# A delta-rule layer with attention and a routed feed-forward: expert gates sent along with the scattered rows, gathers that add, row counts by matmul, softmax sums in PSUM, and a new table of leads

## The chip, the cores and the metric

One core of one Trainium2 chip. The time is device microseconds of one execution of the whole kernel, a median over several runs; one further execution is profiled.

## The reference, cut to what matters

Input x has 4 sequences of 1024 tokens of 128 channels. All arithmetic is float32.

```python
# first half: gated delta rule, 16 heads of 8 channels
q, k, v = silu(depthwise_conv4(silu(x @ W.T)))     # q and k are l2-normalised
a, b = sigmoid(x @ Wa.T), sigmoid(x @ Wb.T)
for t in tokens:                                    # a scan over 1024 steps
    S = a*S - a*b*outer(S @ k, k) + b*outer(v, k)
    o[t] = q @ S
x = layernorm(x + o @ Wo.T)
# second half, on the result
ctx = softmax over the 4 sequences, per token and head   # attention length 4
x   = layernorm(src + ctx @ out_w.T)
probs = softmax(x @ gate_w.T)                       # 8 experts
topv, topi = top_k(probs, 2); topv /= topv.sum()
y = sum over the two chosen e of topv[e] * (relu(x @ w1[e].T + b1[e]) @ w2[e].T + b2[e])
x = layernorm(x + y); x = layernorm(src + x)
```

(Biases are left out; `src` is the result of the first half. The last line stands for the layer norm of the expert part and the residual around the second half.) An expert has 128 inputs, 512 hidden units and 128 outputs.

## The kernel before, in words

The 1024 tokens are cut into 8 chunks of 128 tokens; a chunk holds the same 128 tokens of all four sequences, so most tiles are 128 partitions by 4 x 128 numbers. Each chunk passes through the stages `project` (q, k, v and the gates), `prepare` (convolution, norms, and the triangular solve inside blocks of 8 tokens), `recur` (16 serial steps, one per block), `output`, `attend` (up to the softmax, lines 1325 to 1354), `attended` (the rest of the attention, routing, and the shared part of the result), and `experts`. `experts` runs over the groups (0, 1), (2, 3), (4, 5), (6), (7) of chunks.

One step of `recur` is four VectorE instructions (L1095, L1101, L1110, L1116), with one ScalarE activation (L1107) that the third of them waits for; step n+1 begins with the result of step n, in PSUM.

`attended` makes for each chunk a mask of the two chosen experts per token, the gates `g2`, and `rank`: with one matmul against a triangular matrix the number of earlier tokens of the same sequence that chose each expert (L1455), and with one against ones the number in the whole chunk (L1456), both for each of the four sequences. It also writes `base`, the part of the result that needs no expert, to DRAM (`base_kept`).

`experts` works out for every token and choice a row in a DRAM table `sorted` that has each expert's tokens together, rounded up to tiles of 128 rows: it adds the totals of the sequences (L1500, L1505), derives the first row of each expert, and walks over the sequences, adding `first` to the ranks (L1543) and the sequence's total to `first` (L1545). Eight indirect DMAs per chunk (L1555, on GpSimd's queue) scatter the rows of `x2`, the normalised tokens, into `sorted`. Then it goes over the tiles, four at a time: load four tiles (L1566), transpose them (L1571), apply the layer norm's gain (L1573, `xlT`), and for each tile load the weights of its expert, 514 KB (L1586, three buffers), four matmuls into PSUM `ph` (L1596), four activations into `h` (L1605), four matmuls into PSUM `pm` (L1609). After four tiles one ScalarE copy takes `pm` to `yl` (L1617), which is stored in the DRAM table `ys` (L1618). `ph` and `pm` have one bank each. At the end, per chunk, `acc` is loaded from `base_kept` (L1623), eight indirect DMAs gather rows of `ys` into a buffer `yg` (L1627), and after each one VectorE does acc = yg * gate + acc (L1633). Two layer norms (lines 1244 to 1252), a gain (L1644) and a residual (L1647) follow, and the store of the output.

The order in which each engine gets its instructions is not that of the program. The kernel is built twice: the first time a planner (`plan`, `forward`) gives every instruction a cost and a rank, runs a list schedule over the five queues, and keeps the order; the second time this order is imposed. The rank is the length of the longest chain behind an instruction, plus a number from the table `LEAD`, one for every 60 instructions of a stage. The delay from the end of an instruction to one on another engine is taken from the table `HOP`. Where the planner sees a hole on TensorE, it puts in matmuls whose result is not used (L612), to keep its clock up. DMAs other than the indirect ones are issued by SyncE (SP), in its planned order.

Of the kernel before, what the change touches and what calls it, by code (L numbers as in the profile page):

```python
# [51 lines left out]
T = 128  # L52
# [9 lines left out]
E, F = 8, 512  # L62
# [3 lines left out]
NT = 2 * B * T * GROUP // P + E - 1  # L66
STEPS = B * T * GROUP // P
Q = 4
# [16 lines left out]
class Slots:  # L85
# [32 lines left out]
PE_, DVE_, ACT_, POOL_, SP_ = range(5)  # L118


HOP = (
    (0.0, 0.054, 0.053, 0.054, 0.05, 0.044),
    (0.038, 0.0, 0.033, 0.034, 0.04, 0.03),
    (0.037, 0.035, 0.0, 0.04, 0.04, 0.05),
    (0.09, 0.08, 0.063, 0.0, 0.06, 0.07),
    (0.031, 0.028, 0.026, 0.027, 0.0, 0.017),
)

OVERLAP = (0.0, 0.083, 0.11, 0.043, 0.0)

# [1 line left out]

PIECE = 60
LEAD = (
    (-596, -698,),
    (-695,),
    (1215, 1142,),
    (-239,),
    (-326,),
    (42, 327,),  # L140
    (-717, -154,),
    (-605, -1049,),
    (-810,),
    (-141, -914,),
    (-468,),
    (847, 645,),
    (142, 371,),
    (832, -867,),
    (-1488,),
    (-525, 14,),  # L150
    (21,),
    (154, 573,),
    (-536, 239,),
    (150, -335,),
    (-139, 302, 1084, 833, 618, 867, 306, -62, 535,),
    (-103,),
    (-319, 358,),
    (21,),
    (822, 1113,),
    (325, 133,),  # L160
    (-330, -211,),
    (-341,),
    (-499, -431,),
    (-273,),
    (809, 430,),
    (21, 79,),
    (510, -110,),
    (-99, 422, 15, 260, -43, 347, -211, 876, 125,),
    (-488,),
    (97, -532,),  # L170
    (-438,),
    (334, 1061,),
    (82, -55,),
    (-748, -468,),
    (-347,),
    (-566, -206,),
    (-890,),
    (673, 244,),
    (-525, -84,),
    (-74, -848,),  # L180
    (330, -102, -426, -699, -279, -40, -524, 453, 218,),
    (-566,),
    (129, -1199,),
    (-377, -137,),
    (-533, 514,),
    (378, 91, 339, 237, 165, 545,),
    (172,),
    (-80, 3,),
    (-409, -393, 106, 565, -698, 771,),
)  # L190
WINDOW, DOWN, UP = 3.413, 0.39, 0.77
FILL, FILL_MIN, FILLER = 0.7, 0.5, 0.225
TABLES = {"Silu": 1, "Sigmoid": 2, "Exp": 3}


# [221 lines left out]
def forward(units, rank):  # L417


    q = Queue(units, [u.preds for u in units], rank)  # L420
# [4 lines left out]
    for _ in units:  # L425
# [62 lines left out]
        for s in u.succs:  # L488
            v = units[s]
            if v.engine != e or transfer:  # L490
                q.release(s, end + HOP[v.engine][5 if transfer else e])
            else:
                q.release(s, end if k in v.waits and e != PE_ else begin)
    return begin_, end_, order, holes


# [98 lines left out]
def delta_moe_kernel(  # L595
# [176 lines left out]

    sorted_rows = []
    for n in range(2):
        t = nc.dram_tensor(f"sorted{n}", (NT * P, C), F32).ap()

        sorted_rows.append((t, dram_disjoint_views(t, GROUP * 2 * B)))

    def clear_sorted():
        zero = tile2k("zero", "yl", 2).rearrange("p s c -> p (s c)")  # L780
        nc.vector.memset(zero, 0.0)
        for t, _ in sorted_rows:
            for i in range(0, NT, 4):
                m = min(4, NT - i)
                nc.sync.dma_start(
                    t[i * P : (i + m) * P].rearrange("(i p) c -> p i c", p=P),
                    zero[:, 0 : m * C].rearrange("p (i c) -> p i c", c=C),
                )


# [485 lines left out]
    def attend(c):  # L1276
# [46 lines left out]
        for s in range(B):  # L1323
# [7 lines left out]
                MUL,  # L1331
            )
            prods.append(prod)
        ps = psum.tile([P, B, T // 2], F32, tag="pc", name=f"ps_sc{c}", bufs=1)
        for s in range(B):
            for f in range(2):
                nc.tensor.matmul(  # L1337
# [10 lines left out]
            sc, ps, mx[:, None, :].to_broadcast([P, B, T // 2]), SUB  # L1348
        )
        nc.scalar.activation(sc, sc, AF.Exp, scale=float(DH) ** -0.5)  # L1350
        den = small([P, T // 2], f"den{c}")
        nc.vector.tensor_reduce(den, sc.rearrange("p s t -> p t s"), AX.X, ADD)
        nc.vector.reciprocal(den, den)
        nc.vector.tensor_tensor(
# [4 lines left out]
    def attended(c):  # L1359
# [35 lines left out]
        x2 = tile2k(f"x2_{c}", "x2", 3)  # L1395
# [85 lines left out]
        routed[c] = (x1_kept, base_kept, x2, best, g2, rank)  # L1481

    def pick(best, out, t, name):
        chosen = small([P, 2, B, E], name)
# [5 lines left out]
    def experts(group):  # L1490
# [3 lines left out]
        nt = 2 * B * T * len(group) // P + E - 1  # L1494


        n_e = small([P, E], f"ne{g0}")
        for i, (_, _, _, _, _, rank) in enumerate(members):
            if i == 0:
                nc.vector.tensor_reduce(  # L1500
                    n_e, rank[:, 1].rearrange("p s e -> p e s"), AX.X, ADD
                )
            else:
                more = small([P, E], f"more{g0}")
                nc.vector.tensor_reduce(  # L1505
                    more, rank[:, 1].rearrange("p s e -> p e s"), AX.X, ADD
                )
                nc.vector.tensor_tensor(n_e, n_e, more, ADD)
# [28 lines left out]

        xs, views = sorted_rows[groups.index(group) % 2]
        rows_of_ = []
        for i, (_, _, x2, best, _, rank) in enumerate(members):  # L1540
            where = rank[:, 0]
            for s in range(B):
                nc.vector.tensor_tensor(where[:, s], where[:, s], first, ADD)  # L1543
# [17 lines left out]
        ys = dram.tile([NT * P, C], F32, tag="ys", name=f"ys{g0}")  # L1561
        for i0 in range(0, nt, Q):
            m = min(Q, nt - i0)
            part = slice(i0 * P, (i0 + m) * P)
            xl = tile2k(f"xl{g0}_{i0}", "xl", 2)
            nc.sync.dma_start(  # L1566
                xl[:, 0:m], xs[part].rearrange("(i p) c -> p i c", p=P)
            )
            ps = psum.tile([P, Q, P], F32, tag="ph", name=f"ps_xl{g0}_{i0}", bufs=1)
            for i in range(m):  # L1570
                nc.tensor.transpose(ps[:, i, :], xl[:, i, :], ident)  # L1571
# [45 lines left out]
            nc.scalar.copy(yl[:, 0:m], ps_y[:, 0:m])  # L1617
            nc.sync.dma_start(  # L1618
                ys[part].rearrange("(i p) c -> p i c", p=P), yl[:, 0:m]
            )  # L1620
        for c, (x1_kept, base_kept, _, _, g2, _), rows_at in zip(group, members, rows_of_):
            acc = tile2k(f"acc{c}", "acc", 2)
            nc.sync.dma_start(acc, base_kept)  # L1623
            for g in range(2):
                yg = tile2k(f"yg{c}_{g}", "yg", 1)
                for s in range(B):
                    gp.indirect_dma_start(  # L1627
                        yg[:, s, :],
                        None,
                        ys[0 : nt * P, :],  # L1630
                        bass.IndirectOffsetOnAxis(ap=rows_at[:, g, s : s + 1], axis=0),
                    )
                    nc.vector.scalar_tensor_tensor(  # L1633
                        acc[:, s, :],
                        yg[:, s, :],
                        g2[:, g, s : s + 1],
                        acc[:, s, :],
                        MUL,
                        ADD,
                    )  # L1640
# [198 lines left out]
```

## Time and profile before

| | |
|---|---|
| median of 3 runs | 833.56 us (831.26 to 834.96) |
| the profiled execution | 832.78 us |
| its span, first to last instruction | 831.1 us |
| busy: TensorE (PE) | 699.4 us, 84% of the span |
| busy: VectorE (DVE) | 564.6 us, 68% |
| busy: ScalarE (ACT) | 412.8 us, 50% |
| busy: GpSimd (POOL) | 475.4 us, 57% |
| granted TensorE clock, mean | 0.953 |
| moved | 139.67 MB, mean 168 GB/s |
| last step of the last `recur` | ends at 566 us |
| last matmul of the last expert tile | ends at 802.5 us |

Busy time is that in which an engine has at least one instruction under way; matmuls that only keep the clock up count. PEld is TensorE's loading of weights, which overlaps its matmuls. A float32 matmul leaves two records.

### The profile page before, as it was taken

The numbers are of one execution on the slowest core, as the hardware profiler recorded it, in microseconds if no ns is written. First come the engines' busy times: TensorE is split into PE (matmuls) and PEld (weight loads), VectorE is DVE, ScalarE is ACT, GpSimd is POOL, SyncE is SP. The second block draws the span as 40 slices with busy tenths as digits, with TensorE's granted clock in tenths as the row PEclk, the third lists the DMA queues.
The fourth block names the chain that finished last, engine by engine and source line by source line (L and its number), as shares of the span: only waits on it lengthen the run. The fifth ranks groups of instructions, "written<-read, shape, count | busy, mean of one in ns | idle before, by whom it ended". The sixth has DMA issues, their size and how long they took to land. (4 is left out here: it accounts for less than half of the span.)

```text
span 831.1 us, 15634 instructions
## 1 busy us (share of the span) xinstructions
PE 699.4 (84%) x5000; PEld 516.5 (62%) x5000; DVE 564.6 (68%) x1742; ACT 412.8 (50%) x1163; POOL 475.4 (57%) x656
## 2 busy tenths in 40 slices
PE   8989797889985988999889888799898999977750
PEld 5555545456553673667677577577477878777640
DVE  2167897898977998989899888987426351531303
ACT  5246362555653435486456435455325565465531
POOL 3534339849646748846746987653778621662213
PEclk9999999999997999999989999999899999999995
DMA  7642244252425245378458648568268688788741
GB/s 204 172 136 85 90 128 130 79 178 79 127 89 156 75 148 171 104 218 264 147 175 279 192 124 249 151 193 264 87 203 231 215 231 256 229 243 258 210 124 29
DMA packets 120070, 139.67 MB, mean 168 GB/s; under 512 B 9517, under 2 KB 90933, under 8 KB 119989
## 3 DMA queue, kind: packets, MB, share of 16 engines
q1 hardware_dynamic: 115893, 130.29, 52.0%
q0 software_dynamic: 4096, 8.40, 3.6%
q8 instruction: 39, 0.64, 0.3%
q14 instruction: 42, 0.34, 0.1%
HBM read 99.53 MB, written 39.12 MB: 167 GB/s over the span
## 5 line engine op out<-in xcount | busy, mean ns | idle before, releaser
L1605 ACT ACTIVATE h<-ps_ph,w_e 128x128 f32<-128x128 f32 x396 | 115.0, 368 | 91.2 <-PE ps_ph L1596 46.8
L1609 PE MATMUL ps_pm<-w_e,h 128*128 128x128 f32 x792 | 134.8, 296 | 19.9 <-ACT h L1605 18.6
L1609 PEld LDWEIGHTS ps_pm<-w_e,h 128*128 128x128 f32 x792 | 110.7, 193 | 39.8 <-ACT h L1605 34.9
L1596 PE MATMUL ps_ph<-xlT,w_e 128*128 128x128 f32 x792 | 116.8, 287 | 8.2 <-ACT xlT L1573 4.4
L1596 PEld LDWEIGHTS ps_ph<-xlT,w_e 128*128 128x128 f32 x792 | 101.1, 196 | 21.2 <-ACT xlT L1573 9.3
L897 PE MATMUL ps_pa<-z,diag 128*128 128x512 f32 x192 | 94.3, 620 | 7.8 <-ACT conv L906 3.0
L1627 POOL DMA_INDIRECT yg<-dr_ys,rows_at x64 | 62.2, 972 | 56.1 <-DMA dr_ys<-yl 26.9
L1555 POOL DMA_INDIRECT sorted<-x,rows_at x64 | 63.3, 989 | 49.9 <-DVE rows_at L1551 20.1
L1107 ACT ACTIVATE p<-ps_su,g_block 128x32 f32<-128x32 f32 x127 | 40.3, 317 | 98.4 <-DVE ps_su L1101 95.9
L1201 POOL TENSOR_TENSOR out_work<-sc__0_704,qg_r 128x512 f32<-128x512 f32 x64 | 73.4, 1165 | 14.3 <-PE ps_po L1205 5.7
L1633 DVE SCALAR_TENSOR_TENSOR acc<-yg,g2x,acc 128x128 f32<-128x128 f32 x64 | 24.0, 379 | 72.1 <-DMA yg<-dr_ys,rows_at 71.9
L1110 DVE TENSOR_TENSOR p<-ps_su,kd_r 128x256 f32<-128x256 f32 x127 | 53.1, 418 | 19.2 <-ACT p L1107 18.8
L897 PEld LDWEIGHTS ps_pa<-z,diag 128*128 128x128 f32 x192 | 33.9, 194 | 43.7 <-issue 30.3
L1101 DVE TENSOR_REDUCE ps_su<-z 128x32 f32<-128x288 f32 x128 | 58.1, 454 | 1.9
L1095 DVE TENSOR_TENSOR z<-ps_su,wt 128x256 f32<-128x256 f32 x128 | 53.4, 417 | 8.5 <-ACT su_out L1133 3.9
L1116 DVE TENSOR_REDUCE ps_su<-p 128x32 f32<-128x288 f32 x127 | 57.5, 453 | 1.6
L1173 POOL TENSOR_TENSOR out_work<-uc,q_r 128x192 f32<-128x192 f32 (+3 forms) x64 | 51.0, 827 | 12.3 <-DMA uc<-dr_su_back 11.8
L1219 POOL TENSOR_TENSOR out_work<-k_r,qu 128x128 f32<-128x128 f32 (+6 forms) x64 | 50.7, 818 | 7.8 <-DVE o L1227 5.3
L1086 ACT COPY z<-x 128x32 f32<-128x32 f32 x128 | 30.7, 245 | 38.7 <-DVE ps_su L1101 38.3
L940 POOL TENSOR_TENSOR work<-conv 128x320 f32<-128x320 f32 (+6 forms) x56 | 36.0, 666 | 22.4 <-DVE x L1035 19.5
L1035 DVE TENSOR_REDUCE x<-work 128x128 f32<-128x256 f32 (+6 forms) x56 | 45.5, 812 | 1.2 <-ACT work L1026 0.3
L1252 ACT ACTIVATE acc<-acc,le_nm,le_rs 128x128 f32<-128x128 f32 x64 | 28.1, 496 | 34.0 <-DVE le_nm L1250 34.0
(209 smaller groups left out, 1481.6 us busy)
## 6 DMA issues: line engine op xcount, KB each, us to landing
w_e<-in_wp SPq DMA_DIRECT2D x99, 514.0 KB, 4.7
dr_bounce<-conv SPq DMA_DIRECT2D x24, 256.0 KB, 2.4
xl<-sorted SPq DMA_DIRECT2D x21, 256.0 KB, 3.2
dr_ys<-yl SPq DMA_DIRECT2D x21, 256.0 KB, 5.0
kd_r<-dr_bounce SPq DMA_DIRECT2D x16, 256.0 KB, 3.1
work<-dr_bounce SPq DMA_DIRECT2D x16, 256.0 KB, 4.5
dr_su_back<-su_out SPq DMA_DIRECT2D x8, 512.0 KB
sorted<-yl SPq DMA_DIRECT2D x10, 256.0 KB, 4.3
```

The source lines that it names most:

```text
L897: nc.tensor.matmul(ps, lhsT=diag[:, i, j, :], rhs=z[:, i, :, j : j + T], start=(j == 0), stop=(j == KC - 1),)
L1095: nc.vector.tensor_tensor(z1n[:, :, :, 0:DH], s[:, :, None, :].to_broadcast([P, HD, J, DH]), wt[n // HALF][:, None, here_cut, :].to_broadc ...
L1101: nc.vector.tensor_reduce(u, z1n, AX.X, ADD)
L1110: nc.vector.tensor_tensor(p3[:, :, :, 0:J], u[:, :, None, :].to_broadcast([P, HD, DH, J]), ks[:, None, :, cut].to_broadcast([P, HD, DH, J] ...
L1116: nc.vector.tensor_reduce(ring[:, (n + 1) % (2 * RING), 0 : HD * DH].rearrange("p (d e) -> p d e", e=DH), p3, AX.X, ADD,)
L1173: gp.tensor_tensor(t[:, :, row_of(j) - r0 : row_of(j + 1) - r0], uv[:, :, 0 : j + 1], qv[:, :, j : j + 1].to_broadcast([P, BN, j + 1]), MUL,)
L1201: gp.tensor_tensor(t, sv[:, :, :, d_ : d_ + 1].to_broadcast([P, B, NB, J]), gv, MUL)
L1555: gp.indirect_dma_start(views[(i * 2 + g) * B + s][0 : nt * P, :], bass.IndirectOffsetOnAxis(ap=rows_at[:, g, s : s + 1], axis=0), x2[:, s ...
L1596: nc.tensor.matmul(ps[:, f, :], lhsT=w1[:, f * P : (f + 1) * P], rhs=xlT[:, i, :], start=True, stop=True,)
L1605: nc.scalar.activation(h[:, f, :], ps[:, f, :], AF.Relu, bias=b1[:, f : f + 1])
L1609: nc.tensor.matmul(ps_y[:, i, :], lhsT=h[:, f, :], rhs=w2[:, f, :], start=(f == 0), stop=(f == NF - 1),)
L1627: gp.indirect_dma_start(yg[:, s, :], None, ys[0 : nt * P, :], bass.IndirectOffsetOnAxis(ap=rows_at[:, g, s : s + 1], axis=0),)
```

## The change

- **Gates with the rows.** The rows of `x2` and of `sorted` become 129 numbers long. Before the four scatters of choice g, a ScalarE copy writes the gate of choice g into the last column. For choice 1 this copy has to wait until the four scatters of choice 0 have landed, since they read the same tile. The copy from `pm` to `yl` becomes one activation per tile, with the gate as its scale, so `ys` holds gated rows; `xl` is now needed until then.
- **Gathers that add.** The gathers write into `acc` itself, with an addition in the DMA; the buffer `yg` and the VectorE instruction behind each gather are gone. A gather of choice 1 waits for that of choice 0 on the same rows, and the first for the load of `acc`.
- **Counts over sequences by matmul.** Three more matmuls add the totals of earlier sequences to the ranks, and four in place of one make the chunk's total. In `experts` the walk over the sequences is one broadcast addition, and the two reductions of totals are gone. Two ScalarE copies take `rank` out of PSUM, in place of one on VectorE.
- **Softmax sums in PSUM.** `den` lies in the bank of the scores instead of in SBUF.
- **The planner.** A table `SELF` adds a delay between dependent instructions on one engine, one entry of `HOP` (TensorE after ScalarE) goes from 0.053 to 0.1, and all of `LEAD` is new, so that the order on every engine differs.

```diff
 HOP = (
-    (0.0, 0.054, 0.053, 0.054, 0.05, 0.044),
+    (0.0, 0.054, 0.1, 0.054, 0.05, 0.044),
...
+SELF = (0.0, 0.034, 0.031, 0.05, 0.0)
...
 LEAD = (
-    (-596, -698,),
+    (-367, -625,),
...
-                q.release(s, end if k in v.waits and e != PE_ else begin)
+                q.release(s, end + SELF[e] if k in v.waits and e != PE_ else begin)
...
-        t = nc.dram_tensor(f"sorted{n}", (NT * P, C), F32).ap()
+        t = nc.dram_tensor(f"sorted{n}", (NT * P, C + 1), F32).ap()
...
-        ps = psum.tile([P, B, T // 2], F32, tag="pc", name=f"ps_sc{c}", bufs=1)
+        both = psum.tile([P, B + 1, T // 2], F32, tag="pc", name=f"ps_sc{c}", bufs=1)
+        ps, den = both[:, 0:B], both[:, B]
...
-        den = small([P, T // 2], f"den{c}")
         nc.vector.tensor_reduce(den, sc.rearrange("p s t -> p t s"), AX.X, ADD)
...
-        nc.tensor.matmul(ps[:, 0], lhsT=earlier, rhs=mask, start=True, stop=True)
-        nc.tensor.matmul(ps[:, 1], lhsT=all_ones, rhs=mask, start=True, stop=True)
+        nc.tensor.matmul(ps[:, 0], lhsT=earlier, rhs=mask, start=True, stop=False)
+        for s in range(B - 1):
+            nc.tensor.matmul(
+                ps[:, 0, s + 1 :],
+                lhsT=all_ones,
+                rhs=mask[:, s : s + 1, :].to_broadcast([P, B - 1 - s, E]),
+                start=False,
+                stop=False,
+            )
+        for s in range(B):
+            nc.tensor.matmul(
+                ps[:, 1, 0],
+                lhsT=all_ones,
+                rhs=mask[:, s],
+                start=False,
+                stop=(s == B - 1),
+            )
         rank = small([P, 2, B, E], f"rank{c}", 3)
-        nc.vector.tensor_copy(rank, ps)
+        nc.scalar.copy(rank[:, 0], ps[:, 0])
+        nc.scalar.copy(rank[:, 1, 0], ps[:, 1, 0])
...
-            for s in range(B):
-                nc.vector.tensor_tensor(where[:, s], where[:, s], first, ADD)
-                if i < len(group) - 1 or s < B - 1:
-                    nc.vector.tensor_tensor(first, first, rank[:, 1, s], ADD)
+            nc.vector.tensor_tensor(
+                where, where, first[:, None, :].to_broadcast([P, B, E]), ADD
+            )
+            if i < len(group) - 1:
+                nc.vector.tensor_tensor(first, first, rank[:, 1, 0], ADD)
...
             for g in range(2):
+                nc.scalar.copy(x2g[:, :, C], g2[:, g])
                 for s in range(B):
                     gp.indirect_dma_start(
...
-                        x2[:, s, :],
+                        x2g[:, s, :],
...
-            nc.scalar.copy(yl[:, 0:m], ps_y[:, 0:m])
+            for i in range(m):
+                nc.scalar.activation(
+                    yl[:, i], ps_y[:, i], AF.Copy, scale=xl[:, i, C : C + 1]
+                )
...
-                yg = tile2k(f"yg{c}_{g}", "yg", 1)
                 for s in range(B):
                     gp.indirect_dma_start(
-                        yg[:, s, :],
+                        acc[:, s, :],
                         None,
                         ys[0 : nt * P, :],
                         bass.IndirectOffsetOnAxis(ap=rows_at[:, g, s : s + 1], axis=0),
-                    )
-                    nc.vector.scalar_tensor_tensor(
-                        acc[:, s, :],
-                        yg[:, s, :],
-                        g2[:, g, s : s + 1],
-                        acc[:, s, :],
-                        MUL,
-                        ADD,
+                        compute_op=ADD,
                     )
```

More of the change, by code (lines that the diff above doesn't have):

```diff
@@ L134 @@
 LEAD = (
-    (-596, -698,),
[L136 to L189, printed above, removed]
+    (-367, -625,),
+    (-536,),
+    (1275, 749,),
+    (-495,),
+    (-15,),
+    (189, 487,),
+    (-368, 91,),
+    (-199, -1401,),
+    (-847,),
+    (187, -946,),
+    (40,),
+    (1604, 540,),
+    (-239, 211,),
+    (1003, -1069,),
+    (-1981,),
+    (-323, 289,),
+    (431,),
+    (223, 558,),
+    (-466, 386,),
+    (294, 154,),
+    (-62, 289, 966, 958, 564, 858, 282, -366, 375,),
+    (-269,),
+    (-655, 24,),
+    (-82,),
+    (933, 1259,),
+    (696, 273,),
+    (-172, -361,),
+    (-213,),
+    (-575, -313,),
+    (432,),
+    (1026, 944,),
+    (11, -375,),
+    (328, 16,),
+    (-511, 420, -68, -121, 321, 298, -376, 944, -269,),
+    (-836,),
+    (195, -611,),
+    (-883,),
+    (346, 909,),
+    (-132, -271,),
+    (-1063, -705,),
+    (-493,),
+    (-347, -142,),
+    (-652,),
+    (822, 84,),
+    (-197, 117,),
+    (-269, -954,),
+    (-50, -437, -840, -1170, -530, -474, -730, 873, 46,),
+    (-631,),
+    (316, -1676,),
+    (-154, -165,),
+    (-117, 689,),
+    (852, -114, -92, 309, 172, 279,),
+    (78,),
+    (-440, 397,),
+    (-393, 438, 629, 744, -903, 971,),
 )
 WINDOW, DOWN, UP = 3.413, 0.39, 0.77
-FILL, FILL_MIN, FILLER = 0.7, 0.5, 0.225
+FILL, FILL_MIN, FILLER = .7, 0.5, 0.225
 TABLES = {"Silu": 1, "Sigmoid": 2, "Exp": 3}
@@ L774, in delta_moe_kernel @@
     for n in range(2):
-        t = nc.dram_tensor(f"sorted{n}", (NT * P, C), F32).ap()
+        t = nc.dram_tensor(f"sorted{n}", (NT * P, C + 1), F32).ap()
         sorted_rows.append((t, dram_disjoint_views(t, GROUP * 2 * B)))
     def clear_sorted():
-        zero = tile2k("zero", "yl", 2).rearrange("p s c -> p (s c)")
+        zero = pl.tile([P, Q, C + 1], F32, tag="xl", name="zero", bufs=2)
         nc.vector.memset(zero, 0.0)
@@ L786, in clear_sorted @@
                     t[i * P : (i + m) * P].rearrange("(i p) c -> p i c", p=P),
-                    zero[:, 0 : m * C].rearrange("p (i c) -> p i c", c=C),
+                    zero[:, 0:m],
                 )
@@ L1394, in attended @@
         nc.vector.tensor_tensor(r2, ps_ao, x1, ADD)
-        x2 = tile2k(f"x2_{c}", "x2", 3)
+        x2g = pl.tile([P, B, C + 1], F32, tag="x2", name=f"x2_{c}", bufs=3)
+        x2 = x2g[:, :, 0:C]
         layernorm(r2, x2, "l2")
@@ L1480, in attended @@
         nc.sync.dma_start(base_kept, base)
-        routed[c] = (x1_kept, base_kept, x2, best, g2, rank)
+        routed[c] = (x1_kept, base_kept, x2g, best, g2, rank)
     def pick(best, out, t, name):
@@ L1494, in experts @@
         nt = 2 * B * T * len(group) // P + E - 1
-        n_e = small([P, E], f"ne{g0}")
         for i, (_, _, _, _, _, rank) in enumerate(members):
             if i == 0:
-                nc.vector.tensor_reduce(
-                    n_e, rank[:, 1].rearrange("p s e -> p e s"), AX.X, ADD
-                )
-            else:
[L1504 to L1508, printed above, removed]
+                n_e = rank[:, 1, 0]
+            else:
+                more = small([P, E], f"ne{g0}")
+                nc.vector.tensor_tensor(more, n_e, rank[:, 1, 0], ADD)
+                n_e = more
         n_steps = B * T * len(group) // P
@@ L1539, in experts @@
         rows_of_ = []
-        for i, (_, _, x2, best, _, rank) in enumerate(members):
+        for i, (_, _, x2g, best, g2, rank) in enumerate(members):
             where = rank[:, 0]
-            for s in range(B):
-                nc.vector.tensor_tensor(where[:, s], where[:, s], first, ADD)
-                if i < len(group) - 1 or s < B - 1:
-                    nc.vector.tensor_tensor(first, first, rank[:, 1, s], ADD)
+            nc.vector.tensor_tensor(
[3 more added lines that the diff above has]
+                nc.vector.tensor_tensor(first, first, rank[:, 1, 0], ADD)
             rows_f = small([P, 2, B], f"rowf{g0}")
@@ L1564, in experts @@
             part = slice(i0 * P, (i0 + m) * P)
-            xl = tile2k(f"xl{g0}_{i0}", "xl", 2)
+            xl = pl.tile([P, Q, C + 1], F32, tag="xl", name=f"xl{g0}_{i0}", bufs=2)
             nc.sync.dma_start(
@@ L1570, in experts @@
             for i in range(m):
-                nc.tensor.transpose(ps[:, i, :], xl[:, i, :], ident)
+                nc.tensor.transpose(ps[:, i, :], xl[:, i, 0:C], ident)
             xlT = tile2k(f"xlT{g0}_{i0}", "xlT", 2)
@@ L1631, in experts @@
                         bass.IndirectOffsetOnAxis(ap=rows_at[:, g, s : s + 1], axis=0),
-                    )
-                    nc.vector.scalar_tensor_tensor(
-                        acc[:, s, :],
-                        yg[:, s, :],
-                        g2[:, g, s : s + 1],
-                        acc[:, s, :],
-                        MUL,
-                        ADD,
+                        compute_op=ADD,
                     )
```

## The prediction

> **What bounds the kernel now.** I read the slices of the span first, then cut the span where their pattern changes. The view of busy time by stretches shows three regimes (columns: stretch, its length, busy time and count per engine, granted clock, DMA share, GB/s):
>
> ```profile
> 80.00:566.00 486.00, 422.69 (x3104) 298.75 (x3102) 431.32 (x1234) 249.71 (x726) 315.61 (x429) 0.95 0.51 155
> 566.00:803.00 237.00, 205.53 (x1512) 174.15 (x1511) 90.58 (x356) 120.24 (x353) 113.16 (x127) 0.98 0.73 217
> 803.00:831.10 28.10, 0.00 (x0) 0.00 (x0) 7.58 (x28) 3.33 (x9) 10.11 (x12) 0.57 0.13 35
> ```
>
> From 80 to 566 us the scan over the chunks runs, and VectorE is busy 431 of 486 us (89%). TensorE's 423 us contain 68 us of unused matmuls (L612), so it isn't the limit there. From 566 to 803 us the remaining expert tiles run and TensorE is busy 206 of 237 us (87%), 15 us of it unused; VectorE only 91. The last 28 us are a chain of latencies. The waits of VectorE and ScalarE inside the first stretch (total, times, longest) say how loose it is:
>
> ```profile
> ACT p L1107 <- DVE ps_su L1101: 95.5, 54, 12.1
> DVE p L1110 <- ACT p L1107: 18.2, 39, 1.1
> DVE kd_r L1014 <- DMA kd_r<-dr_bounce: 9.9, 1, 9.9
> ```
>
> ScalarE waits for VectorE far more than VectorE for ScalarE. VectorE waits only 18.2 us for the recurrence's own activation, and once 9.9 us for a load. That load was late because SyncE, which issues it, stood 10.80 us in one store (the others of that line take 0.38), as the timeline has it (start, us):
>
> ```profile
> 237.33 10.80 SPq L1139 DMA_DIRECT2D dr_su_back<-su_out  x1
> ```
>
> In the second stretch the waits are:
>
> ```profile
> DVE acc L1633 <- DMA yg<-dr_ys,rows_at: 42.3, 20, 12.5
> ACT h L1605 <- PE ps_ph L1596: 31.4, 18, 3.2
> PEld ps_pm L1609 <- ACT h L1605: 25.8, 46, 2.4
> ```
>
> VectorE's 42.3 us at L1633 cost nothing here, since it has slack; the two others alternate, TensorE and ScalarE handing `ph` and `h` to each other, about 2.5 us a tile.
>
> **Removed from VectorE before 566 us.** The groups, kept apart by form (busy us, mean ns | idle before):
>
> ```profile
> L1633 DVE SCALAR_TENSOR_TENSOR acc<-yg,g2x,acc 128x128 f32<-128x128 f32 x64 | 24.0, 379 | 72.1 <-DMA yg<-dr_ys,rows_at 71.9
> L1543 DVE TENSOR_TENSOR rank<-rank,first 128x8 f32<-128x8 f32 x32 | 5.1, 160 | 0.2
> L1354 DVE TENSOR_TENSOR sc<-sc,den 128x256 f32<-128x256 f32 x8 | 6.6, 826 | 0.0
> L1347 DVE TENSOR_TENSOR sc<-ps_pc,mx 128x256 f32<-128x256 f32 x8 | 3.3, 415 | 0.1
> L1431 DVE TENSOR_TENSOR prod<-pb 128x256 f32<-128x256 f32 x8 | 3.3, 418 | 0.0
> ```
>
> - Gathers that add: 16 of the 64 L1633 lie before 566 us, 7.2 us.
> - Row counts: 16 of L1543 and 14 of L1545 lie there. They start 0.20 us apart (571.56, 571.74, 571.95 in the timeline), so 30 x 0.20 = 6.0; four broadcast additions and two of `first` stay, about 1.2. Gone: 4.8.
> - Five copies of `rank` at 214 ns go to ScalarE: 1.1. Five reductions of totals (L1500, L1505) at about 0.2: 1.0.
> - Softmax: L1354 ranges from 396 to 1580 ns; the six before 566 us take 5.8. With `den` in PSUM only one operand is read from SBUF, as in L1347, which takes 415. 6 x 0.415 = 2.5; gone 3.3. Bounds: 0 (each stays as it is) to 3.4 (each at 396). The sum and reciprocal before it (598 and 540 ns) now write PSUM; the steps of the recurrence that write PSUM (L1101) are not dearer than their size, so 0.
>
> [...]
>
> Sum 17.4. Laying the two instruction orders side by side with row means, VectorE has 12.7 us less work ahead of the last step of `recur` before the softmax gain, so 16.0 with it; something else moved forward. VectorE's share was 0.89 and freed time uncovers waits for L1107, so I take 0.8 of 16: **-13**. Bounds: 0 (below, under B) and -17.
>
> **Added before 566 us.** Per chunk six more rank matmuls, 0.22 us each by L1455 (0.41 for two): 36 make 7.9 us. They lie in TensorE's 63 idle us and in place of unused matmuls: 0, or +7.9 if that cover is gone. ScalarE (51% busy) gets ten rank copies, eight gate copies, and four activations per `yl`. A gate copy of choice 1 waits for four scatters to land and holds everything behind it in ScalarE's queue, L1107 of the recurrence too. The scatters (L1555) take 2.7 to 6.4 us from issue to landing, median 4.8, and are issued 1.26 us apart. In the groups of two chunks the new order puts the other chunk's four scatters between, 5.04 us: about the landing time. Taken +1; bounds 0 and 4 x 6.4 - 4 x 5 = 6.
>
> The planner's new order: the multiplication L1014 that waited 9.9 us has 9.7 and 12.6 us of VectorE work ahead of it in the two chunks that may meet that stall, against 7.8 and 8.4: **-2**. Bounds: -9.9 if the stall misses, 0 if not helped.
>
> **566 to 803 us.** Twelve rank matmuls (chunks 6, 7) on the busiest engine: +2.6 (bounds 0 and 2.6). The end of a group of four tiles shows in the timeline (start, us, engine, line, then in brackets the wait):
>
> ```profile
> 716.17 0.58 ACT L1617 COPY yl<-ps_pm 128x512 f32<-128x512 f32 x1
> 716.58 1.16 PE L1596 MATMUL ps_ph<-xlT,w_e 128*128 128x128 f32 x8
> 717.83 1.14 ACT L1605 ACTIVATE h<-ps_ph,w_e 128x128 f32<-128x128 f32 x4 [1.08 <-issue]
> ```
>
> Four activations of 128 columns take 1.14 us where the copy takes 0.58: +0.56 per group, and right behind it ScalarE is idle for 1.08 us, waiting for `ph`. So hidden: +0, or 14 groups x 0.56 = 8 if that cover is gone; +1 taken. `xl` is now held until `yl`, but its reload is issued some 8 us ahead. Gate copies: chunks 4 and 5 have the other chunk's scatters between, chunk 7 only two gathers (2.5 us against 3.1 to 4.9 landing here), chunk 6 little; +2 (0 to 10). The expert tiles ahead of the end of the scan are 40.5 in the new order, 40.8 in the old: 0.3 x 2.5 = +0.7. Sum **+6.3**. The removed L1633 and count additions give nothing in this stretch.
>
> **The last 28 us.** After the last gather one L1633 (0.36) and its semaphore go; the last `yl` (384 columns, 0.48) is three activations, about 0.85. What adding in the DMA costs a gather no row shows: the nearest are plain gathers, 2.5 us issue to landing at the end and 5.5 at worst. Two are chained (choice 1 after choice 0), but four issues of 1.26 us lie between. Bounds -0.4 and +3; I take **+0.4**, since paced issue hides a small excess.
>
> Sum: 831.1 - 13 + 1 - 2 + 6.3 + 0.4 = 823.8 span. The profiled run was 1.7 longer than its span, 832.8, and 0.8 below the median: as a median 823.8 + 1.7 + 0.8 = 826.3; I give **826**.
>
> **Rivals.** *A* is the sum above. Its own range goes from the stall gone (-7.9) to half of the -13 lost (+6.5): 818 to 833.
>
> *B, no change, 833.* The scan needs four VectorE instructions a step (417 + 454 + 418 + 453 ns) and L1107 (317 ns) in the middle. VectorE covers that activation with other work in all but the 39 waits. What goes was part of that cover: if 0.4 of 16 reaches the path, that is -6.4, and with the additions of 1 + 6.3 + 0.4 and the -2 it gives 833.6 - 6.4 + 7.7 - 2 = 832.9. For it: waits of mean 0.47 us already in a third of the steps. Against: some 230 us of other VectorE work remain for it.
>
> *C, slower, 848.* ScalarE's queue stands at the choice-1 gate copies. At 3.1 us (a short landing of this trace) eight of them cost 25, less the 3 that the sum has: 826 + 22 = 848. From 1.3 us each the gain is gone ((7.6 + 3)/8), from 1.9 us ((7.6 + 3 + 4.2)/8) it is slower by 0.5%. For it: GpSimd issues the scatters among its own 1.2 us multiplications, so that they land later than 5 us after the first, and behind the copy stands L1107. Against: the other chunk's scatters in six of eight. Dearer adding gathers end on the same side.
>
> *D, better, 814:* the SyncE stall does not recur (9.9 in place of the 2), the waits for `p` don't grow (0.89 of 16, 1.2 more), and the gate copies are covered (3): 826 - 7.9 - 1.2 - 3 = 813.9.
>
> That the sums might not be what they seem, such as `den` in PSUM not being faster, is worth 3 us and inside A.
>
> **How the numbers follow.** A 0.42, B 0.20, C 0.24, D 0.14. A difference of 0.5% (4.2 us, bounds 829.4 and 837.7) is about what a measurement of this kernel can tell from no change. Faster by more: most of A (0.38), D, and a little of B (0.05): 0.57. Same: 0.04 of A, 0.13 of B, 0.03 of C: 0.20. Slower: 0.21 of C and 0.02 of B: 0.23. The range leaves out a tenth on either side: the better part of D (beyond 814 by the 2.6 of hidden rank matmuls) and the worse half of C (below 848 by one gate copy of 3.1): 811 to 845.
>
> **What would show it.** Right: VectorE busy some 410 in the scan, its end near 552 instead of 566 us, the first stretch shorter, the second up to 6 us longer, L1354's successor near 415 ns, no ScalarE wait over 2 us for a scatter. Wrong: waits "gate copy <- DMA" of 3 us with L1110 waiting behind (C), L1110's wait grown from 18 to near 30 us (B), gathers that land later than 5 us, or a new wait of SyncE or of TensorE for ScalarE at `ph`.

## The result and the profile after

884.15 us median (879.39 to 896.47) against 834.26 (831.26 to 836.05): 1.0578 of the time before, 95% interval 1.0517 to 1.0639. The ratio is that of executions in the common, faster state, so without the slowest one after (896.47), which ran at a lower granted clock (0.907; the others 0.919 to 0.929). The change is slower by 50 us; the forecast was faster by 8. The profiled execution has a span of 881.3 us (831.1 before). The view of stretches, cut at the kernel's own marks (last step of the scan, last matmul), in the columns of before:

```profile
0.00:80.00 80.00, 66.95 (x350) 40.06 (x351) 29.18 (x111) 34.59 (x66) 36.36 (x88) 0.96 0.63 149
80.00:584.50 504.50, 434.69 (x3172) 305.31 (x3170) 428.46 (x1193) 260.44 (x775) 325.61 (x429) 0.94 0.50 146
584.50:849.00 264.50, 220.31 (x1579) 191.50 (x1578) 76.38 (x291) 133.19 (x422) 136.37 (x127) 0.92 0.71 201
849.00:881.30 32.30, 0.00 (x0) 0.00 (x0) 4.77 (x20) 3.29 (x8) 14.83 (x12) 0.53 0.18 30
```

All three stretches lost. The scan ends at 584.4 instead of 565.6 us (+18.8), the expert tiles behind it take 264 instead of 237 (+27), the last part 32.3 instead of 28.1 (+4). VectorE's work did shrink, from 564.6 to 538.8 us in the whole span, but in the scan its share fell from 89 to 85%: it waits more. The granted clock behind the scan fell from 0.98 to 0.92. Added up from the trace's clock records up to the last matmul, TensorE ran 112.6 us at half clock, 54.6 before; in the stretch of the expert tiles 44.4, 10.2 before.

The groups that answer to those shown of before:

```profile
L1648 POOL DMA_INDIRECT acc<-dr_ys,rows_at x64 | 99.8, 1560 | 53.8 <-DMA dr_ys<-yl 21.5 <-issue 18.1 <-DMA w_e<-in_wp 10.2
L1357 DVE TENSOR_TENSOR sc<-sc,ps_pc 128x256 f32<-128x256 f32 x8 | 3.3, 412 | 0.1
L1559 DVE TENSOR_TENSOR rank<-rank,first 128x32 f32<-128x32 f32 x8 | 1.4, 170 | 0.0
L1637 ACT ACTIVATE yl<-ps_pm,xl 128x128 f32<-128x128 f32 x99 | 29.0, 369 | 3.2 <-PE ps_pm L1628 3.1
L1572 ACT COPY x<-g2x 128x4 f32<-128x4 f32 x16 | 3.2, 199 | 14.1 <-DVE g2x L1510 9.4 <-DMA sorted<-x,rows_at 4.6
```

The removed VectorE work, the softmax product at 412 ns, and the price of a gate copy are as forecast. The copies' waits for landed scatters come to 4.6 us in all, so rival C as it was priced is not the cause; the 9.4 us in which copies waited for VectorE to make the gate were in no sum. The surprise is in the first line: a gather that adds holds GpSimd for 1.56 us, a plain one 0.97.

**Where it shows in the scan.** In the timeline, GpSimd issues thirteen of these in a row, 1.86 us apart, and only then the multiplication L1175 that TensorE's L1183 needs; VectorE's L1190 waits, and behind it in VectorE's queue the next step of the recurrence (L1097):

```profile
525.89 1.55 POOL L1648 DMA_INDIRECT acc<-dr_ys,rows_at  x1 [0.30 <-issue]
527.75 1.55 POOL L1648 DMA_INDIRECT acc<-dr_ys,rows_at  x1 [0.30 <-issue]
528.74 5.54 POOL L1175 TENSOR_TENSOR out_work<-uc,q_r 128x192 f32<-128x192 f32 x7
530.90 0.55 PE L1183 MATMUL ps_po<-out_work,head_sum 128*32 128x96 f32 x8 [6.49 <-POOL out_work L1175]
531.51 0.26 DVE L1190 TENSOR_TENSOR qu<-ps_po,dq 128x96 f32<-128x96 f32 x1 [4.88 <-PE ps_po L1183]
531.69 0.41 DVE L1097 TENSOR_TENSOR z<-ps_su,wt 128x256 f32<-128x256 f32 x1
```

The waits of VectorE between 80 and 584.5 us:

```profile
DVE p L1112 <- ACT p L1109: 27.0, 51, 1.7
DVE qu L1190 <- PE ps_po L1183: 16.7, 4, 8.2
DVE z L1097 <- ACT su_out L1135: 8.1, 11, 2.3
```

The wait for `p` grew from 18.2 to 27.0 us, that for `qu` from 1.7 to 16.7, that for `su_out` from 3.9 to 8.1: 28 us more. Of the 15 for `qu`, 7.7 follow the gathers above. The longest, 8.2, follows a load in whose issue SyncE stood for 10 us:

```profile
248.12 10.06 SPq L1159 DMA_DIRECT2D uc<-dr_su_back  x1
```

This is the stall of before, then in L1139 and felt at `kd_r`; it has only moved. Against the 28 us stand the 9.9 us at `kd_r` that are gone and 9 us less VectorE work ahead of the scan's end (35.2 + 431.3 before, 29.2 + 428.5 after). The other 9 us, and the 6 of the start, are most of the scan's 18.8.

**Where it shows at the start.** Clearing the table `sorted`, with rows of 129 numbers, holds SyncE's queue longer, and the loads behind it are late. First the kernel after, then before:

```profile
12.09 10.23 SPq L787 DMA_DIRECT2D sorted<-xl  x8
23.88 3.17 SPq L787 DMA_DIRECT2D sorted<-xl  x2
32.74 0.33 SPq L1163 DMA_DIRECT2D k_r<-dr_bounce  x1
```

```profile
11.93 5.73 SPq L785 DMA_DIRECT2D sorted<-yl  x8
22.59 1.07 SPq L785 DMA_DIRECT2D sorted<-yl  x2
24.58 0.33 SPq L1161 DMA_DIRECT2D k_r<-dr_bounce  x1
```

The median landing of one such store grew from 4.3 to 9.3 us (258 KB instead of 256), and the recurrence begins at 73.2 instead of 66.8 us.

**Where it shows in the expert tiles.** The prediction counted VectorE's waits for gathers in this stretch as costless. In the kernel after they reach TensorE. VectorE stands at the layer norm of a gathered tile (L1246) until an adding gather has landed; the gate that it makes behind that is late; ScalarE stands at the copy of this gate; and behind the copy in ScalarE's queue is `xlT`, for which TensorE waits:

```profile
750.10 0.29 DVE L1246 BATCH_NORM_STATS2 le_st<-acc 128x6 f32<-128x128 f32 x1 [5.42 <-DMA acc<-dr_ys,rows_at]
751.46 0.22 DVE L1510 TENSOR_REDUCE g2x<-pickg 128x8 f32<-128x64 f32 x1
751.71 0.20 ACT L1572 COPY x<-g2x 128x4 f32<-128x4 f32 x1 [6.08 <-DVE g2x L1510]
751.81 0.77 ACT L1592 ACTIVATE xlT<-ps_ph,ln 128x512 f32<-128x512 f32 x1
752.64 2.08 PE L1615 MATMUL ps_ph<-xlT,w_e 128*128 128x128 f32 x8 [5.05 <-ACT xlT L1592]
```

Some 75 us later the activation of another such layer norm (L1254) waits 4.88 us at the head of ScalarE's queue, again with `xlT` behind it, and TensorE waits 6.30 us. Before, TensorE's longest wait of this stretch was 2.75 us. The two waits make 11.4 us, and TensorE is idle 12.7 us longer in this stretch (44.2 instead of 31.5). It is also busy 14.8 us longer. The clock was halved from 752.0 to 758.8 and from 823.7 to 830.5 us, beside both waits: the eight matmul records above took 2.08 us, the eight of the same line at 743.35 us took 1.06. From these two times I estimate that a stretch at half clock costs at most half of its length, so the 34 us more of it can explain the 14.8. `after_again` shows the first of these chains too: 5.21 us at the copy, 4.17 us for TensorE.

### The profile page after: what moved, and what is told of

It is laid out like the page before. It is cut to its first block, busy times and chain, and to the rows that moved or that the text cites. A ratio compares the mean times of both kernels' runs of the same rounds, so it can differ in the third digit from the quotient of the medians.

```text
span 881.3 us, 15804 instructions
## 1 busy us (share of the span) xinstructions
PE 721.9 (82%) x5098; PEld 536.9 (61%) x5098; DVE 538.8 (61%) x1614; ACT 431.5 (49%) x1268; POOL 513.2 (58%) x656
## 5 line engine op out<-in xcount | busy, mean ns | idle before, releaser
L1615 PE MATMUL ps_ph<-xlT,w_e 128*128 128x128 f32 x792 | 126.4, 301 | 23.2 <-ACT xlT L1592 16.3
L1628 PEld LDWEIGHTS ps_pm<-w_e,h 128*128 128x128 f32 x792 | 112.9, 199 | 36.3 <-ACT h L1624 32.1
L1648 POOL DMA_INDIRECT acc<-dr_ys,rows_at x64 | 99.8, 1560 | 53.8 <-DMA dr_ys<-yl 21.5
L1615 PEld LDWEIGHTS ps_ph<-xlT,w_e 128*128 128x128 f32 x792 | 109.0, 208 | 35.6 <-ACT xlT L1592 19.5
L899 PE MATMUL ps_pa<-z,diag 128*128 128x512 f32 x192 | 99.7, 647 | 10.7 <-ACT z L852 5.9
L1203 POOL TENSOR_TENSOR out_work<-sc__0_701,qg_r 128x512 f32<-128x512 f32 x64 | 74.9, 1215 | 23.1 <-PE ps_po L1207 13.5
L1246 DVE BATCH_NORM_STATS2 le_st<-acc 128x6 f32<-128x128 f32 x64 | 16.2, 285 | 98.2 <-DMA acc<-dr_ys,rows_at 97.9
L1175 POOL TENSOR_TENSOR out_work<-uc,q_r 128x192 f32<-128x192 f32 (+3 forms) x64 | 51.7, 890 | 25.7 <-DMA uc<-dr_su_back 23.5
L1097 DVE TENSOR_TENSOR z<-ps_su,wt 128x256 f32<-128x256 f32 x128 | 53.6, 419 | 13.1 <-ACT su_out L1135 8.1
L1221 POOL TENSOR_TENSOR out_work<-k_r,qu 128x192 f32<-128x192 f32 (+6 forms) x64 | 51.7, 894 | 1.7 <-DVE o L1229 1.6
L1254 ACT ACTIVATE acc<-acc,le_nm,le_rs 128x128 f32<-128x128 f32 x64 | 27.2, 490 | 43.9 <-DVE le_nm L1252 43.9
```

The lines of the kernel that those rows point to most:

```text
L899: nc.tensor.matmul(ps, lhsT=diag[:, i, j, :], rhs=z[:, i, :, j : j + T], start=(j == 0), stop=(j == KC - 1),)
L1097: nc.vector.tensor_tensor(z1n[:, :, :, 0:DH], s[:, :, None, :].to_broadcast([P, HD, J, DH]), wt[n // HALF][:, None, here_cut, :].to_broadc ...
L1175: gp.tensor_tensor(t[:, :, row_of(j) - r0 : row_of(j + 1) - r0], uv[:, :, 0 : j + 1], qv[:, :, j : j + 1].to_broadcast([P, BN, j + 1]), MUL,)
L1203: gp.tensor_tensor(t, sv[:, :, :, d_ : d_ + 1].to_broadcast([P, B, NB, J]), gv, MUL)
L1615: nc.tensor.matmul(ps[:, f, :], lhsT=w1[:, f * P : (f + 1) * P], rhs=xlT[:, i, :], start=True, stop=True,)
L1628: nc.tensor.matmul(ps_y[:, i, :], lhsT=h[:, f, :], rhs=w2[:, f, :], start=(f == 0), stop=(f == NF - 1),)
```

## Experiments

Each run is compared with the kernel before on the same chip. That kernel's own time differs: it took 834 and 835 us where the first comparison and the runs `all_old_order`, `all_new_order` and `hop_self` were made, and 881 to 884 us beside all others. Ratios stand beside the time that before had there.

Theory N, in its wider form O: the numbers, or any edit, make the planner write a new order, and the order is what costs. Theory E: the edits themselves cost; G: the adding gathers, R: the wide rows.

**The numbers alone, and the edits alone.**

```diff
 # new_numbers: the kernel before
-HOP, LEAD = old
+HOP, SELF, LEAD = new
 # old_numbers: the kernel after
-HOP, SELF, LEAD = new
+HOP, LEAD = old
```

> The kernel before with the new planner numbers (HOP, SELF, LEAD) and nothing else. Theory N (the loss of 50 us is the new order: the leads of one program do not suit another): 20 us or more slower than before, with the end of recur 0 already 8 to 12 us late, since the change has hardly begun to run there. Theory G (the loss is the gathers that add, 1.84 us apart instead of 1.26): within 8 us of before. Theory R (the rows of 129 numbers make the loads and the clearing of the table slow): within 8 us, and recur 0 ends on time at 113 us.

> The kernel after with the old planner numbers (old HOP, SELF of zeros, old LEAD); the four edits of the code stay. Theory N: most of the loss is gone, 825 to 845 us. Theories G and R: it stays at 870 us or more, with gathers that take 1.55 us on GpSimd and, under R, recur 0 ending at 120 us or later.

New numbers in the old code: 0.9942 (0.9902 to 0.9982), beside 882. Old numbers in the new code: 1.0363 (1.0282 to 1.0444). So on this chip the new numbers are no loss, and the simple form of theory N is wrong: the edits lose 3.6% with one table and, from the next two runs on another chip, about 2.5% with the other (1.0195 / 0.9942).

> The kernel before, unchanged, for a trace beside those of the other runs, which took 880 us for it where the first runs took 833. If the surroundings differ (clock or memory), the trace shows which lines grew: under a lower clock the matmuls, under slower memory or a slower hand-over the waits and landings. If 833 comes back, the earlier call was disturbed.

> The kernel after, unchanged, timed beside the kernel before again. If the first comparison holds, the ratio is 1.05 to 1.065. If it was made of two different surroundings, the ratio is 0.98 to 1.02: about what my sum said. Old numbers in the kernel after gave 916 beside 882, new numbers in the kernel before 875: so between 0.99 and 1.04 if order and code add up.

Before again: 880 us, span 878.5; after again: 1.0195 (1.0137 to 1.0254) of it. The loss holds, but is 17 us instead of 50 where the kernel before has 881.

**One part each, with a free plan.** Each is the kernel before with that part's hunks of the diff and the old numbers:

```diff
 # gather_add: indirect_dma_start(acc[:, s, :], ..., compute_op=ADD), no VectorE instruction, gates left out
 # wide_rows:  rows of C + 1, gate copies, one activation per tile into yl; gathers into yg, acc = yg + acc
 # counts:     the seven rank matmuls, one broadcast addition per chunk
 # den:        ps, den = both[:, 0:B], both[:, B]
```

> The kernel before with gathers that add into acc, old numbers. The gates are left out of the result. Theory G: 64 gathers of 0.6 us more on GpSimd, 40 of them in the last third, where they hold up scatters and layer norms: 15 to 30 us slower than before, the last eight gathers 1.84 us apart. Theory N: the issues cost 0.6 us each only at the end, 8 x 0.58 = 5 us, so 0 to 8 us slower; a re-planned order may add some us either way.

> The kernel before with the gates in the rows (129 numbers), one activation per tile into yl, and the gathers still into yg, with a plain addition on VectorE. Old numbers. Theory R: 10 to 25 us slower, recur 0 ends at 120 us or later since the clearing of the table takes 9 us a piece instead of 4, and xl lands after 5.0 us instead of 3.2. Theories N and G: within 8 us of before.

> The kernel before with the counts over sequences by matmul alone, old numbers. My sum: VectorE loses 6.9 us in the scan, TensorE gains 48 matmuls; -5 to +2.6 us. If any small edit spoils an order that was found for another program (theory N), 10 us or more slower.

> The kernel before with the softmax sums in PSUM alone, old numbers: no instruction is added or removed. My sum: L1354 at 410 ns in place of 826 on average, -3 us. Theory N: a changed order, 5 us or more slower, though there is nothing slower in it.

Measured: adding gathers 1.019 (1.0101 to 1.0278), wide rows 0.9995 (0.9951 to 1.0038), counts 1.0238 (1.0175 to 1.0301), sums in PSUM 1.0122 (1.0064 to 1.0179). The 17 us of `gather_add` are what theory G expected; of theory R's 10 to 25 us for `wide_rows` nothing came. Two parts that take work from VectorE cost 1.2 and 2.4% (`counts` also gives TensorE 48 matmuls). `den` is the plainest case: no instruction of the work is added or removed, and none is more than 25 ns slower. Yet, comparing the instruction sequences by name, only 57% of TensorE's and 64% of VectorE's order is that of before, and the planner put in 367 unused matmuls instead of 343.

**The same parts, every instruction held in its old place.** The plan is made from the unchanged code and imposed on the edited one:

```diff
 # den_pinned
-        den = small([P, T // 2], f"den{c}")
+        den = small([P, T // 2], f"den{c}") if planned is None else both[:, B]
 # adding_pinned (writing_pinned: the same without compute_op)
-                yg = tile2k(f"yg{c}_{g}", "yg", 1)
+                yg = tile2k(f"yg{c}_{g}", "yg", 1) if planned is None else acc
+                        **({} if planned is None else {"compute_op": ADD}),
 # three_pinned: both of these, and CW = C if planned is None else C + 1 for the rows
```

> The kernel before with the softmax sums in PSUM, as in the earlier single part that took 1.2% more, but with the order of before kept on every engine. Theory O: the 1.2% are gone and 0 to 4 us are gained. If the place in PSUM is itself what costs, it stays 6 us or more slower.

> The kernel before, its order on every engine kept as it was (the plan is taken from the unchanged code), but the gathers add into acc in the DMA instead of writing yg, and the VectorE instruction behind each stays, on acc alone. The result is not the layer's: the gates and sums differ. Theory G (a gather that adds occupies GpSimd for 1.55 us, 1.86 to the next, instead of 0.95 and 1.26; queued work of the scan waits behind it): slower than its twin without the addition by 10 to 25 us. Theory O (the loss comes of the changed order alone): within 6 us of the twin, the last eight issues apart.

> The twin: the same order and the same waits, gathers write acc without adding (the loaded base is overwritten, so the result is not the layer's). The wait of the first gather for the load of acc is new against the kernel before: 0 to 4 us slower than before under either theory.

> The kernel before, every instruction in its old place on every engine, with three parts of the change: rows of 129 numbers (the gate is left out and rows are shifted by a number), gathers that add into acc (the VectorE instruction behind each stays, on acc alone), softmax sums in PSUM. The result is not the layer's. Theory O (the order is what costs): within 1% of before. Theory E (the edits cost): 2% or more slower, from GpSimd's 64 x 0.6 us and from tables that are cleared at 9 us a piece.

`den_pinned` 1.0012 (0.9971 to 1.0053): the 1.2% came of the new plan, and no gain can be told where I had counted 3 us (the interval is -2.6 to +4.7 us). `adding_pinned` 1.0012 (0.9973 to 1.005), its twin 1.0065 (1.0024 to 1.0105): no cost of the addition can be told in that order, although each gather held GpSimd for 1.55 us there too. Theory G by itself falls. `three_pinned` 1.012 (1.005 to 1.019): together the three parts do cost, about 10 us. Line by line against `before_again` (same places, same engines) it lags 4 us from the first loads on, and 7.5 us more at one instruction; at the end it lags 20. But this execution took 900 us, where the median of the run is 889, so not all of that lag is in the 10 us. This is VectorE's timeline at the instruction in `three_pinned`, then the same instruction in `before_again`, and then GpSimd's timeline in `three_pinned`:

```profile
365.35 7.73 DVE L1251 SCALAR_TENSOR_TENSOR l_nm<-l_mv,l_rs 128x4 f32<-128x4 f32 x1
373.00 0.41 DVE L1111 TENSOR_TENSOR p<-ps_su,kd_r 128x256 f32<-128x256 f32 x1
```

```profile
358.33 0.22 DVE L1250 SCALAR_TENSOR_TENSOR l_nm<-l_mv,l_rs 128x4 f32<-128x4 f32 x1
```

```profile
364.90 2.34 POOL L941 TENSOR_TENSOR work<-conv 128x128 f32<-128x128 f32 x4
368.10 1.25 POOL L1008 TENSOR_TENSOR x<-kh,nbg 128x512 f32<-128x512 f32 x1
372.27 1.43 POOL L999 TENSOR_TENSOR coef<-decay,nb 128x96 f32<-128x96 f32 x5
```

An instruction on four numbers a partition takes 7.73 us, while GpSimd runs two-operand work without a break; the recurrence's L1111 stands behind it. GpSimd's work alone does not explain it: in nine of the profiled executions the instruction began at the same place, 82 to 110 ns into the second `work<-conv` of this series. In six it took 0.20 to 0.22 us, `before_again` among them, and in three 7.70 to 7.73: `three_pinned`, `wide_rows` and `all_old_order`. All three have rows of 129 numbers, but why that should matter here is not shown, and `wide_rows` as a whole was not slower (0.9995). In `three_pinned` sixteen GpSimd instructions ended before VectorE's did; what VectorE waited for is not shown.

The counts, the gate copies and the activation per tile were never run in the old order.

**Orders without an edit.**

```diff
 # hop_self: the kernel before with
-    (0.0, 0.054, 0.053, 0.054, 0.05, 0.044),
+    (0.0, 0.054, 0.1, 0.054, 0.05, 0.044),
+SELF = (0.0, 0.034, 0.031, 0.05, 0.0)
 # jitter: the kernel before, LEAD entries +2, -2, +2, ...
```

> The kernel before with HOP and SELF alone, old LEAD: not one instruction of the work differs, only the order. Theory O: 1 to 3% slower, like the single parts, since LEAD belongs to the plan that the old numbers gave. Theory E: within 0.7%.

> The kernel before with 2 added to or taken from each of the 122 numbers of LEAD, in turn, nothing else: only the order differs. Theory O: 1 to 3.5% slower, as hop_self. Theory E: within 0.7%.

> The new numbers in the unchanged code once more; beside before at 881 they took 0.994. Theory O: beside before at 835 they are 2 to 5% slower, since the old order is that much better there; beside 881, 0.99 to 1.0 again. Theory E: 0.99 to 1.0 in either case.

`hop_self`: 1.0348 (1.0284 to 1.0411), beside 835. Not one instruction of the work differs, and some 29 us are lost, with 52% of VectorE's order kept; the planner put in 417 unused matmuls instead of 343. Its scan ends at 590.5 us, later than that of the kernel after (stretches):

```profile
80.00:590.50 510.50, 443.69 (x3192) 312.36 (x3190) 438.63 (x1229) 249.33 (x711) 315.28 (x429) 0.93 0.46 145
590.50:831.00 240.50, 212.06 (x1576) 182.78 (x1576) 93.82 (x361) 125.26 (x370) 112.58 (x127) 0.98 0.71 219
```

`jitter` 1.0042 (0.9995 to 1.0088), beside 882, with 86% of VectorE's order kept: theory O, which expected 1 to 3.5%, missed. `new_numbers_b` 0.9931 (0.9889 to 0.9972), beside 882: the same gain as at first. So a new order can cost, gain a little or change nothing that can be told. The new numbers in the old code are the best version seen there, ahead of both kernels; beside 835 they were not run.

**All edits, near the old order.** Instructions that both programs have keep their planned place, new ones go where their inputs are ready:

```diff
 # all_old_order, all_new_order: the kernel after
-        order, _, times = plan(units, groups)
+        order, fill = follow(units, groups, plan_of_before)   # with old, with new numbers
```

> All four edits of the code, but no plan of their own: the plan of the kernel before is made first, and every instruction that both programs have keeps its place in it; the new ones go where their inputs are ready, and what waits for a scatter moves behind it. Theory O (the new order is what costs): within 1% of before, or up to 1.5% faster, as my sum said. Theory E (the edits themselves cost): 1.5 to 4% slower, like the kernel after (2.0%) and the edits with the old numbers (3.6%).

> The same, with the plan that the new numbers (HOP, SELF, LEAD) give the code of before, which took 0.994 of before. Theory O: 0.98 to 1.0 of before. Theory E: 1.01 or more.

1.1123 (1.1069 to 1.1177) and 1.091 (1.0845 to 1.0974), beside 835: far worse than either kernel, and outside what either theory expected. 91% of VectorE's order was kept in the first, but what waits for scatters was pushed back within an order made for other delays; its `p` wait is 33.8 us, 40.6 us of ScalarE's waits at `h` have no releaser in the trace. So nearly the old order is not a cure, and these two do not separate edits from order.

**The edits with plain gathers.**

```diff
 # after_plain: the kernel after
-                        compute_op=ADD,
+                    nc.vector.tensor_tensor(acc[:, s, :], yg[:, s, :], acc[:, s, :], ADD)
```

> The kernel after, new numbers, with plain gathers into yg and a plain addition on VectorE behind each. Theory G: 12 to 25 us faster than the kernel after (898 beside 881 for before), so 873 to 886, GpSimd pace 1.26 us again. Theory O: no better than after, 892 to 905, since VectorE gets 64 additions back and the order changes again.

1.0315 (1.0244 to 1.0385), beside 884: slower than the kernel after (1.0195), not faster, so theory G's forecast failed: taking the adding gathers out is no cure. Since the planner made a new order here as well, this does not price them.

## Why the prediction was wrong

- **VectorE's work.** The single terms were right: L1357 at 412 ns, 170 ns for the additions that stay, 25.8 us less in all. Ahead of the scan's end, however, VectorE's busy time fell by 8.9 us, not by 16. The step that failed is the factor 0.8 with which freed work was taken to the path (-13). The scan ended 18.8 us later, and three kinds of wait had grown by 28 us; in `den_pinned` 3 us of freed work brought nothing that can be told, and in new orders `den` and `counts` were slower.
- **The planner's new order**, put at -2 us with bounds of -9.9 and 0. This term was bounded on one side, and `hop_self` shows in its place what its size can be: +29 us for a new order without any edit. I had looked at one wait that the order would shift, not at all the others that fit the old one. Rival B named the right kind of loss (its wait for `p` grew to 27.0 us, near the 30 it gave) but had 0.4 of the gain survive.
- **Adding gathers**, +0.4 us at the end with a bound of 3. Eight of them, 1.85 us apart, cost about 8 x 0.59 = 4.7 us, less the 0.4 of the removed L1633: the +4 measured. I had bounded the landing and left out GpSimd's own time, 0.59 us each. In the scan, 7.7 us of VectorE's waits follow a row of thirteen.
- **Wide rows**, priced at nothing: 6 us at the start of the scan, 4 of them in `three_pinned`, where the order is held.
- **The expert stretch**, +6.3, was +27. The step that failed is that VectorE's waits for gathers "cost nothing here", with the gate copies priced by the landing of scatters alone. ScalarE's queue stood once at a gate copy and once at a layer norm that waited for late gathers, and TensorE waited 11.4 us behind them. The sum also took the clock as given: 34 us more at half clock are worth up to 17 by the estimate from 2.08 and 1.06 us.
- **Rival C** had ScalarE's queue stand at gate copies, which it did, but for another reason and less: 4.6 us for scatters and 9.4 for gates, not 25. Rival D fell too: the SyncE stall came again, two DMA issues on.

What is shown: one new order without an edit cost 3.5% where before takes 835 (two others, where it takes 882, changed it by +0.4 and -0.7%), and three edits held in place cost 1.2% where it takes 882. What stays open is the division of the 5.8% between edits and order, since the new numbers in the old code and the pinned parts were not run where before takes 835.

## What to carry to other kernels

Where the order of instructions comes from a planner with a searched table, an edit is two changes, and the smaller one is in the diff: hold the old order to price the edit, and change the table without an edit to price the order. Freed time on the busiest engine may be worth nothing, as the 3 us of `den_pinned` that brought nothing that can be told; look which engine's queue hands over next. A wait on an engine with slack is free only as long as no other engine's queue stands at what it makes afterwards: here TensorE waited 11.4 us behind two such stands. Price a DMA that also computes by what its issuing engine is held (here 1.56 us a gather in place of 0.97), not only by its landing.

## What the runs showed of the hardware

The same program, instruction for instruction, took 831 us of span in one series of runs and 878 in another. Of the five series whose chip is on record no two share one, so it is not shown that the chip makes the difference and not the hour. Busy times agree within 0.2% on VectorE, ScalarE and GpSimd (564.6 and 564.5 us on VectorE); 41 of the 47 us lie behind the scan, where the granted clock is 0.91 instead of 0.98:

```profile
571.50:850.00 278.50, 216.17 (x1518) 183.78 (x1517) 91.64 (x358) 120.91 (x357) 113.33 (x127) 0.91 0.62 185
```

TensorE's longest waits there were 6.3 and 5.4 us between 566 and 660 us and 13.5 between 700 and 800, where those of the faster trace were 2.7 and 2.2. By the timeline of `before_again`, beside the wait of 5.4 us, a result that TensorE had written by 616.3 us is taken up by VectorE at 621.3:

```profile
615.23 1.06 PE L1366 MATMUL ps_pc<-sc,spread 128*128 128x256 f32 x2
621.34 0.69 DVE L1374 TENSOR_TENSOR prod<-ps_pc,kv 128x512 f32<-128x512 f32 x1 [12.47 <-remote]
```

The trace there also holds a quarter fewer landing records, the semaphore updates that DMAs make (6,481 and 8,445). All twenty traces divide this way: the five that belong to a before of 834 or 835 us hold 8,445 to 8,490, the fifteen others 6,398 to 7,303. The kernel after, with 8,481, is of the first sort, so I take its 50 us for no difference of this kind. What delays the hand-over was not found.

SyncE's stall of some 10 us belongs to no line. In 19 of the 20 profiled executions SyncE stood 7.4 to 11.5 us in a DMA issue, once per execution, between 237 and 256 us, and always in its 129th to 134th DMA issue of 405, whatever DMA stood there (four different ones); in `counts` alone it did not (its longest was 3.7 us, the 137th). In these runs an order only chose which DMA was hit.
